# A graph layer on one core: TensorE takes over more of the gather, with 10 sets of nodes instead of 7 and index rows that come from DRAM

## The chip, the cores and the metric

The kernel runs on one core of a Trainium2 chip. The metric is the device time of one launch in microseconds (us); before the change it is 1440.02 us, the median of three runs (1439.52 to 1440.55).

The engines that matter: PE (TensorE, matrix products into PSUM), DVE (VectorE), ACT (ScalarE), POOL (GpSimd, which here issues indirect DMAs) and SP (SyncE, which issues ordinary DMAs). Each works through its own queue in order, and waits for the others by semaphores.

## What is computed

A layer of a graph network with 6250 nodes of 64 features and 206250 edges that are sorted by the node they lead to (`dst`):

```python
h = jnp.maximum(_layernorm(x, axis=-1), 0.0)
msg = jax.nn.relu(h[src] + edge_attr)
agg = jax.ops.segment_sum(msg, dst, num_segments=6250)
h = h + agg
h = jax.nn.relu(h @ W1 + b1)
out = x + h @ W2 + b2
```

The costly parts are `h[src]`, which picks 206250 rows of 256 bytes in no order, and the sum over the edges of each node.

## The kernel before

**Groups.** The edges are cut into 201 groups of 1024 (`NG`, `GE`) and a tail. A group is 128 partitions by 8 columns (`G`), so one column is 128 edges. The loop at L553 runs over the groups; two groups, an even and an odd one, are a pair `k`. The instructions stand in the order in which the code writes them; only semaphores let one engine run ahead of another.

**Two ways to gather.** For most columns POOL issues one indirect DMA each (`gather`, L156), which brings 128 rows of `h_rows` from DRAM into `xg`. In the pairs 2 to 99 (`K0`, `K1`) some columns are left to TensorE: 3 of 8 in even groups, 2 of 8 in odd ones (`EVEN`, `ODD`), `T = 5` per pair, 640 edges. This way goes in stages, a pair or two ahead of use:

- Once, at the start (`ranks`, L231): the source nodes of these edges are split into 7 parts (`SB`) of 7 blocks of 128 nodes, and each edge gets a place among the edges of its pair that have the same part. `hp` holds the node features in SBUF, as three bf16 pieces that add up to f32, 192 columns.
- `hold` (L377, DVE): a one-hot matrix from edge to place. `source` (L387, PE; L389, ACT): products with it give, for each place and part, the source node as a 16-bit number, with the places down the partitions.
- `spread` (L395, PE): transposes that turn a column of such numbers into a row that stands in every partition, in PSUM. It is done for the sources (7) and for the places of the edges, `spot` (5).
- `find` (L403, DVE): 7 comparisons of 128x896 that make the one-hot matrices `found`, from node to place. `back` (L410, DVE): 7 comparisons of 128x640 that make `backs`, from place to edge.
- `slots_of` (L417, PE; L421, ACT): 49 products of `found` with `hp`, added up per part, put the picked rows at their places, `picked`. `pick` (L439, PE): 7 products per column of `backs` with `picked` bring them to the edges, in PSUM beside a copy of the edge attributes (`room`, L430, ACT).

**Messages and sums.** `take` (L481, ACT) copies the attributes of a group to PSUM (`full`); `messages` adds the gathered rows (L489, DVE), folds the three pieces and the attributes of the picked columns into it (L491, DVE), and ACT applies the relu (L494). `one_hot` (L465, DVE) compares each edge's node, counted from the first of its group, with 64 numbers (`W`), and `window_sum` (L503, PE) adds the messages of a group into a window of 64 nodes. `sum_into_z` (L460, DVE) adds the window to `z`, two groups later (`LAG`). Whenever 512 nodes of `z` are done (`blocks_behind`), the two layers follow (L511, L524) and the result is stored (L534).

**Queues and buffers.** `load` issues the attributes on SP (L147) and the gathers on POOL for the next group. `ea` and `xg` have 10 buffers (`LOOK`), so POOL's queue can be up to ten groups ahead of the messages. Of the eight PSUM banks `rows` has one, `pick` two, `turned` two, and `wslots`, `full` and `agg` one each.

## Time and profile before

| | |
|---|---|
| profiled execution, whole run | 1440.22 us |
| its span, first to last instruction | 1438.5 us |
| mean granted TensorE clock | 0.958 |
| gathers (L156), us on POOL | 1036.8 from `h_rows`, 41.2 from `x` |
| `slots_of` (L417), us on PE | 487.7 for 4802 products |
| `pick` (L439), us on PE | 326.2 for 3430 products |
| `window_sum` (L503), us on PE | 234.8 for 3224 |
| `find` (L403), us on DVE | 414.1 for 686 comparisons, 675 ns each |
| `back` (L410), us on DVE | 322.6 for 686, 542 ns each |
| `hold` (L377) and `one_hot` (L465), us on DVE | 79.4 and 136.9 |
| mean traffic of the DMA engines | 71 GB/s |

The times of an engine's groups can be added up against the span; consecutive instructions overlap a little, so the mean duration times the count is more than the busy time. A line of the order of time gives the start in us from the span's start, the duration in us, the engine, the line of the kernel, the operation, the tiles written and read, how many were merged, and in brackets the idle time before it and what ended that. In the list of waits stand the waiting engine and line, the one waited for, the total in us, the number of times and the longest.

### The profile page before, as it was taken

The page shows a single profiled execution, that of the slowest core. Times are in us where ns is not written, and L with a number is a line of the kernel's source. Part 1 is how long each engine was busy: PE and PEld are TensorE (multiplying, and loading weights), DVE is VectorE, ACT ScalarE, POOL GpSimd, SP SyncE. Part 2 cuts the span into 40 slices and gives each one's busy share as a digit, 9 for nine tenths or more (in the row PEclk, how much of TensorE's full clock was granted, in tenths as well). Part 3 has the DMA queues.
Part 4 walks back from the last instruction along what each step waited for, and adds up shares of the span by engine and source line. Part 5 has one row for each costly group of instructions (what it writes and reads, how often), then busy time and mean ns, then how long its engine had stood idle before and what let it go on. Part 6 is the DMA issues. An engine that isn't in the chain of part 4 may idle for free. (4 is left out here: it accounts for less than half of the span.)

```text
span 1438.5 us, 34730 instructions
## 1 busy us (share of the span) xinstructions
PE 1150.1 (80%) x13824; PEld 1015.8 (71%) x13824; DVE 1298.3 (90%) x2546; ACT 478.2 (33%) x1253; POOL 1079.6 (75%) x1131
## 2 busy tenths in 40 slices
PE   1448788888888888888889888888878888888774
PEld 0237677877777777777778777777767777777773
DVE  6889999999999999999999999998988998999972
ACT  2323233333333333333333333333333333333331
POOL 7877777777777777777777777777777777777774
PEclk9959899999999999999999999999999999999995
DMA  5332213214214214214214214214213213311411
GB/s 174 75 98 64 59 29 105 75 28 120 68 28 119 61 28 126 60 28 123 57 28 127 61 28 126 54 28 119 68 28 111 68 29 101 82 32 33 129 28 24
DMA packets 80069, 101.68 MB, mean 71 GB/s; under 512 B 29692, under 2 KB 35964, under 8 KB 79900
## 3 DMA queue, kind: packets, MB, share of 16 engines
q0 software_dynamic: 35904, 36.84, 13.3%
q1 hardware_dynamic: 42748, 60.85, 13.2%
q8 instruction: 110, 1.80, 0.5%
q10 hardware_dynamic: 1248, 1.70, 0.3%
q14 instruction: 59, 0.48, 0.1%
HBM read 96.10 MB, written 3.20 MB: 69 GB/s over the span
## 5 line engine op out<-in xcount | busy, mean ns | idle before, releaser
L156 POOL DMA_INDIRECT xg<-h_rows,src_sb x1090 | 1036.8, 951 | 332.2 <-issue 279.2
L417 PE MATMUL rows<-hp,found 128*128 128x192 bf16 x4802 | 487.7, 250 | 27.7 <-DVE found L403 27.6
L417 PEld LDWEIGHTS <-found 128*128 128x128 bf16 x4802 | 390.7, 99 | 61.8 <-DVE found L403 44.8
L403 DVE TENSOR_SCALAR found<-turned,ids 128x896 bf16<-128x896 int16 x686 | 414.1, 675 | 2.1 <-PE turned L395 2.1
L439 PE MATMUL pick<-picked,backs 128*128 128x192 bf16 x3430 | 326.2, 251 | 111.0 <-ACT pick L430 110.3
L439 PEld LDWEIGHTS <-backs 128*128 128x128 bf16 x3430 | 296.8, 99 | 136.4 <-issue 124.2
L421 ACT CAST picked<-rows 128x384 bf16<-128x384 f32 (+1 forms) x392 | 170.8, 436 | 516.2 <-PE rows L417 513.0
L410 DVE TENSOR_SCALAR backs<-turned,ids 128x640 bf16<-128x640 int16 x686 | 322.6, 542 | 0.0
L503 PE MATMUL agg<-oh,msg 128*64 128x64 f32 x3224 | 234.8, 227 | 44.0 <-DVE z L460 43.5
L503 PEld LDWEIGHTS agg<-oh,msg 128*64 128x64 f32 x3224 | 206.7, 140 | 89.2 <-DVE z L460 57.9
L491 DVE TENSOR_REDUCE full<-pick 128x128 f32<-128x512 f32 (+1 forms) x294 | 179.6, 611 | 43.0 <-PE pick L439 4.8
L494 ACT ACTIVATE msg<-full 128x512 f32<-128x512 f32 x202 | 120.7, 598 | 198.9 <-DVE full L491 182.2
L489 DVE TENSOR_TENSOR full<-full,xg 128x320 f32<-128x320 f32 (+1 forms) x202 | 105.6, 523 | 56.0 <-DMA xg<-h_rows,src_sb 43.6
L465 DVE TENSOR_TENSOR oh<-slot,wslots 128x512 f32<-128x512 f32 x202 | 136.9, 678 | 0.0
L481 ACT COPY full<-ea 128x320 f32<-128x320 f32 (+1 forms) x202 | 92.7, 459 | 22.3 <-DMA ea<-in_edge_attr_dram 16.3
L377 DVE TENSOR_TENSOR holds<-place,wslots 128x640 bf16<-128x640 f32 x98 | 79.4, 811 | 0.0
L430 ACT COPY pick<-ea 128x128 f32<-128x128 f32 (+1 forms) x294 | 65.6, 244 | 0.0
L395 PE MATMUL turned<-ident_b,sources 128*128 128x128 bf16 x686 | 57.4, 227 | 6.5 <-ACT sources L389 5.2
L395 PEld LDWEIGHTS <-sources 128*128 128x128 bf16 x686 | 43.2, 101 | 18.8 <-ACT sources L389 5.5
L389 ACT CAST sources<-rows 128x7 int16<-128x7 f32 x98 | 16.4, 167 | 120.6 <-PE rows L387 113.3
L156 POOL DMA_INDIRECT xg<-in_x_dram,src_sb x32 | 41.2, 1287 | 11.0 <-issue 9.4
L395 PE MATMUL turned<-ident_b,spot 128*128 128x128 bf16 x490 | 45.0, 225 | 0.0
(99 smaller groups left out, 404.0 us busy)
## 6 DMA issues: line engine op xcount, KB each, us to landing
ea<-in_edge_attr_dram SPq DMA_DIRECT2D x201, 256.0 KB
xg<-h_rows,src_sb POOLq DMA_INDIRECT x1090
x_sb<-in_x_dram SPq DMA_DIRECT2D x4, 384.0 KB
h_rows<-ln_h SPq DMA_DIRECT2D x4, 384.0 KB
h_nodes<-h_rows SPq DMA_DIRECT2D x2, 768.0 KB
xb<-in_x_dram SPq DMA_DIRECT2D x12, 128.0 KB
out_dram<-o SPq DMA_DIRECT2D x12, 128.0 KB
dst_sb<-in_dst_main_dram ACTq DMA_DIRECT2D x1, 804.0 KB
```

Source lines behind the costliest of these rows:

```text
L156: nc.gpsimd.indirect_dma_start(out=xg[:, j, :], out_offset=None, in_=rows[:, :], in_offset=bass.IndirectOffsetOnAxis(ap=idx[:, j:j + 1], a ...
L395: nc.tensor.transpose(row[:, i], col[:, i:i + 1].bitcast(BF16).to_broadcast([P, P]), ident_b)
L403: nc.vector.tensor_scalar(found[k][:, b], row, ids[:, b:b + 1], None, op0=ALU.is_equal)
L410: nc.vector.tensor_scalar(backs[k][:, m], row, ids[:, m:m + 1], None, op0=ALU.is_equal)
L417: nc.tensor.matmul(ps[:, i], found[k][:, b, m + i, :], hp[:, (m + i) * SB + b].rearrange("p t d -> p (t d)"), start=(b == 0), stop=(b == S ...
L421: nc.scalar.copy(picked[k][:, m:m + n], ps[:, :n])
L439: nc.tensor.matmul(pk[:, u, :3].rearrange("p t d -> p (t d)"), backs[k][:, m, t0 + i + u, :], picked[k][:, m], start=(m == 0), stop=(m == ...
L465: nc.vector.tensor_tensor(oh[:, :n], slot[:, cols_of(g)].unsqueeze(2).to_broadcast([P, n, W]), wslots[:, :W].unsqueeze(1).to_broadcast([P, ...
L489: nc.vector.tensor_tensor(full[:, :m], full[:, :m], xg[:, :m], ALU.add)
L491: nc.vector.tensor_reduce(full[:, m + i:m + i + c], pk[:, :c].rearrange("p j t d -> p j d t"), AX.X, ALU.add)
L494: nc.scalar.activation(msg[:, :n], full[:, :n], AF.Relu)
L503: nc.tensor.matmul(pa, msg[:, j, :], oh[:, j, :], start=(j == 0), stop=(j == n - 1))
```

## The change

TensorE gets 4 columns of even groups and 2 of odd ones; POOL keeps 4 and 6. The nodes are split into 10 parts of 625, each 5 blocks of 125. The rows that are compared are no longer made by transposes into PSUM: the places (`spot`) of all pairs are turned once at the start and stored in DRAM, and the sources of a pair are computed with the places along the row, stored in DRAM, and read back into every partition, 16 bits each. `find` becomes 5 comparisons of 125x1280, `back` 10 of 128x768, `slots_of` 50 products, `pick` 10 per column. A small `mask` per pair (two operations on DVE) takes the place of the arrays `part_n` and `part_b`. The banks of `turned` go to `rows` (2) and `pick` (3). The window has 48 nodes, `slot` is 16-bit, the window starts are read 16 at a time. Loads enter six groups ahead (`AHEAD`), with nine buffers. In the loop the comparisons stand ahead of the messages.

The diff, cut to its core:

```diff
-W = 64
+W = 48
-LOOK = 10
+LOOK = 9
+AHEAD = 6
-SB = 7
-KB = SB * SB
-PART = SB * P
-EVEN, ODD = 3, 2
+SB, BB, BN = 10, 5, 125
+KB = SB * BB
+PART = BB * BN
+EVEN, ODD = 4, 2
-RV = 8
+RV = 16
...
     def ranks(pool):
...
-        for m in range(SB):
-            nc.vector.tensor_tensor(part_n[:, m], mine[:, m], src_f, ALU.mult)
-            nc.vector.tensor_tensor(part_b[:, m], mine[:, m], block, ALU.mult)
...
+        for c in range(0, KS * T, P):
+            n = min(P, KS * T - c)
+            turned = psum.tile([P, P], BF16, name="rows", bufs=2)
+            nc.tensor.transpose(turned[:n], spot[:, c:c + n].bitcast(BF16), ident_b)
+            sp = pool.tile([P, P], BF16, name="sp", bufs=2)
+            nc.scalar.copy(sp[:n], turned[:n])
+            nc.sync.dma_start(out=spot_rows[c:c + n, :], in_=sp[:n])
...
-    slot = const.tile([P, C + CT], F32, name="slot")
+    slot = const.tile([P, C + CT], I16, name="slot")
...
+    def mask(k):
+
+        at = hot.tile([P, T, SB], BF16, name="at", bufs=1)
+        nc.vector.tensor_tensor(at, part[:, k - K0].unsqueeze(2).to_broadcast([P, T, SB]),
+                                of_part.unsqueeze(1).to_broadcast([P, T, SB]), ALU.is_equal)
+        mk = hot.tile([P, T, 2, SB], BF16, name="mask")
+        nc.vector.tensor_tensor(mk, at.unsqueeze(2).to_broadcast([P, T, 2, SB]),
+                                node[:, k - K0].unsqueeze(3).to_broadcast([P, T, 2, SB]), ALU.mult)
+        masks[k] = mk
+
     def source(k):
 
-        oh = holds.pop(k)
-        ps = psum.tile([P, SB], F32, name="rows", bufs=1)
+        oh, mk = holds.pop(k), masks.pop(k)
+        ps = psum.tile([SB, P], F32, name="rows", bufs=2)
         for t in range(T):
-            for i, a in enumerate((part_n, part_b)):
-                nc.tensor.matmul(ps, oh[:, t, :], a[:, :, k - K0, t], start=(t + i == 0), stop=(t == T - 1 and i == 1))
-        sources[k] = hot.tile([P, SB], I16, name="sources")
-        nc.scalar.copy(sources[k], ps)
-
-    def spread(k, col, n):
-
-        row = psum.tile([P, SB, P], BF16, name="turned", bufs=2)
-        for i in range(n):
-            nc.tensor.transpose(row[:, i], col[:, i:i + 1].bitcast(BF16).to_broadcast([P, P]), ident_b)
-        return row
+            for i in range(2):
+                nc.tensor.matmul(ps, mk[:, t, i, :], oh[:, t, :], start=(t + i == 0), stop=(t == T - 1 and i == 1))
+        col = hot.tile([SB, P], I16, name="source")
+        nc.scalar.copy(col, ps)
+        line = dram.tile([SB, P], I16, name="source_row", bufs=3)
+        nc.sync.dma_start(out=line, in_=col)
+        sources[k] = hot.tile([P, SB * P], I16, name="sources")
+        nc.sync.dma_start(out=sources[k], in_=line.rearrange("(o m) s -> o (m s)", o=1).to_broadcast([P, SB * P]))
+
+    def spot(k):
+
+        spots[k] = hot.tile([P, T * P], BF16, name="spots")
+        nc.sync.dma_start(out=spots[k], in_=spot_rows[(k - K0) * T:(k - K0 + 1) * T, :]
+                          .rearrange("(o t) s -> o (t s)", o=1).to_broadcast([P, T * P]))
 
     def find(k):
 
-        row = spreads.pop((k, "source")).bitcast(I16)
-        found[k] = hot.tile([P, SB, SB, P], BF16, name="found")
-        for b in range(SB):
-            nc.vector.tensor_scalar(found[k][:, b], row, ids[:, b:b + 1], None, op0=ALU.is_equal)
+        row = sources.pop(k)
+        found[k] = hot.tile([P, BB, SB, P], BF16, name="found")
+        for b in range(BB):
+            nc.vector.tensor_scalar(found[k][:BN, b].rearrange("p m s -> p (m s)"), row[:BN], ids[:BN, b:b + 1], None,
+                                    op0=ALU.is_equal)
 
     def back(k):
 
-        row = spreads.pop((k, "spot"))[:, :T].bitcast(I16)
+        row = spots.pop(k).bitcast(I16)
         backs[k] = hot.tile([P, SB, T, P], BF16, name="backs")
         for m in range(SB):
-            nc.vector.tensor_scalar(backs[k][:, m], row, ids[:, m:m + 1], None, op0=ALU.is_equal)
+            nc.vector.tensor_scalar(backs[k][:, m].rearrange("p t s -> p (t s)"), row, ids[:, m:m + 1], None,
+                                    op0=ALU.is_equal)
...
+    for g in range(AHEAD):
+        enter(g)
     take(0)
+    for k in (K0, K0 + 1):
+        spot(k)
     hold(K0)
+    mask(K0)
     for g in range(NG + 1):
         k, even = g // 2, g % 2 == 0
+        now = is_set(k + 1)
+        enter(g + AHEAD)
         if g >= LAG:
             sum_into_z(g - LAG)
             blocks_behind(g - LAG)
+        if even:
+            if now:
+                slots_of(k + 1, 0, 2)
+                slots_out(k + 1, 0, 2)
+                back(k + 1)
+            if is_set(k + 2):
+                source(k + 2)
+            if is_set(k + 3):
+                spot(k + 3)
+        else:
+            if now:
+                slots_of(k + 1, 6, 2)
+                slots_out(k + 1, 6, 2)
+                slots_of(k + 1, 8, 2)
+                slots_out(k + 1, 8, 2)
+            if is_set(k + 2):
+                find(k + 2)
+            if is_set(k + 3):
+                hold(k + 3)
         if g < NG:
             room(g + 1)
         if g >= 1:
             window_sum(g - 1)
+        if now and even:
+            for m in (2, 4):
+                slots_of(k + 1, m, 2)
+                slots_out(k + 1, m, 2)
+        messages(g)
+        take(g + 1)
         if g < NG and is_set((g + 1) // 2):
             pick(g + 1)
+        if even and is_set(k + 3):
+            mask(k + 3)
         one_hot(g)
```

`slots_out` is the copy by ACT that stood at the end of `slots_of`. The lines that this order replaces are left out of the diff: before, `messages` and `take` stood ahead of `room` and `window_sum`, and `source`, `back`, `find` and `hold` after `pick`.

## The prediction

> **What bounds the kernel now.** I read the page's busy line first, then the groups by line and shape, then POOL's waits, then the order of time at the start, in the middle and at the end.
>
> ```profile
> PE 1150.1 (80%) x13824; PEld 1015.8 (71%) x13824; DVE 1298.3 (90%) x2546; ACT 478.2 (33%) x1253; POOL 1079.6 (75%) x1131
> L156 POOL DMA_INDIRECT xg<-h_rows,src_sb x1090 | 1036.8, 951 | 332.2 <-issue 279.2 <-DMA xg<-h_rows,src_sb 33.2 <-DVE found L403 11.0
> POOL xg L156 <- issue: 288.6, 947, 0.3
> ...
> 1420.68 0.94 POOL L156 DMA_INDIRECT xg<-h_rows,src_sb  x1 [0.30 <-issue]
> 1421.06 0.70 DVE L489 TENSOR_TENSOR full<-full,xg 128x512 f32<-128x512 f32 x1 [8.27 <-DMA xg<-h_rows,src_sb]
> ...
> 1423.18 0.94 POOL L156 DMA_INDIRECT xg<-h_rows,src_sb  x1 [0.30 <-issue]
> ```
>
> DVE has the largest share, yet POOL is the bound. A gather lies on POOL for 0.94 us and the next begins 0.30 us after it: a spacing of 1.249 us. No wait of POOL's own is longer than 0.3 us ("issue"), apart from one of 1.5 us at the start. The first gather starts at 4.50 us, the last ends at 1424.12. 1122 gathers (1090 + 32) at 1.249 make 1401.4 us; the stretch is 1419.6. So POOL is never free: 18.2 us of longer gathers are all that is left. DVE waits 8.27 us for gathered rows near the end. After the last gather come 14.4 us of tail (1438.5 - 1424.1), and the run of the profile took 1.7 us more than its span (1440.22 against 1438.5; the median of the runs, 1440.02, is the same within 0.02%).
>
> In quiet stretches DVE and PE turn a pair of groups in 12.61 us (`found` begins at 710.60 and 723.21), where POOL needs 11 gathers, 13.74 us. They work off the lead that POOL has at the start, and then wait.
>
> **Fewer gathers.** A pair goes from 11 gathers to 10; 98 pairs save 98 x 1.249 = 122.4 us on the engine that sets the end. 1024 gathers make 1279.0 us.
>
> **What DVE's new comparisons do to POOL.** This decides. `found` and `backs` read PSUM today, and the gathers beside them take 0.94 us. Afterwards they read 16-bit rows in SBUF and write SBUF. The loop of before has no such row, but its first 55 us do:
>
> ```profile
> 42.10 2.42 DVE L251 TENSOR_SCALAR mine<-part 128x490 bf16<-128x490 f32 x7
> 42.24 1.07 POOL L156 DMA_INDIRECT xg<-in_x_dram,src_sb  x1 [0.30 <-issue]
> 43.61 1.06 POOL L156 DMA_INDIRECT xg<-in_x_dram,src_sb  x1 [0.30 <-issue]
> ...
> 46.12 0.66 DVE L254 TENSOR_TENSOR part_n<-mine,src_f 128x490 bf16<-128x490 bf16 x1
> 46.24 8.90 POOL L156 DMA_INDIRECT xg<-in_x_dram,src_sb  x1 [0.31 <-issue]
> ...
> 53.65 0.67 DVE L255 TENSOR_TENSOR part_b<-mine,block 128x490 bf16<-128x490 bf16 x1
> ```
>
> Two kinds of streak, both SBUF to SBUF. Under seven tensor-scalars back to back (2.42 us) two gathers lose 0.12 us each: each is held to the end of the operation that was running and slips in before the next. Under fourteen tensor-tensors with two SBUF inputs one gather is shut out until the whole streak is over: 8.90 us instead of 0.94. The new comparisons are tensor-scalars, like L251; L254 is the other bound.
>
> Their length first. From 490 to 1612 f32 elements a tensor-scalar within SBUF goes from 0.413 us (L251) to 0.995 (L339): 0.52 ns an element and 0.16 us fixed. Out of PSUM, 16-bit elements run at 0.52 ns (L410 to L403: 542 to 675 ns for 256 more) where f32 runs at 1.05 (L465: 410 to 679 ns for 256 more). Halving the element halves its time there, so I take 0.26 ns for 16 bits in SBUF: 0.49 us for 1280 elements, 0.36 us for 768. Consecutive ones start some 0.07 us closer than they last (L403: 4.23 us for seven of 0.675), so `found` is 5 x 0.42 = 2.1 us (before 4.23) and `backs` 10 x 0.29 = 2.9 us (3.29). If nothing halves, they are 3.8 and 4.9 us.
>
> Now the loss of POOL per pair. By L251's share (0.244 of 2.42 us, 10%), 5.0 us of comparisons and 0.5 us of `mask` (two tensor-tensors with two SBUF inputs) cost 0.56 us. By half an operation for each gather that lands there (2.1/1.25 x 0.21 + 2.9/1.25 x 0.145 + 0.05) it is 0.74. I take 0.65, or 64 us in 98 pairs: both events of L251 met the operation at the same point, so neither figure is better. The ends: 0, and the L254 kind. There a gather meets a streak after 0.62 us on average and waits for the rest: (2.1 - 0.62) + (2.9 - 0.62) + 0.05 = 3.8 us per pair.
>
> The Trainium skill speaks against the change here ("SBUF — State Buffer", "Who interferes with whom"): a Vector operation in a two-port mode and a GpSimd operation shut each other out for the whole instruction, and tensor-scalars within SBUF can take that mode. Read so, all 5.0 us of comparisons would be lost to POOL in each pair and the sum below would come to about 1321 + 98 x 5.0 = 1811 us. The L251 rows contradict this reading: three more operations of the streak ran over the rest of the first gather, and it lost only 0.12 us.
>
> **DVE and PE, beside POOL.** DVE per pair after: `found` 2.1, `backs` 2.9, `holds` 0.95 (0.81 at 640 elements, 128 more at 1.05 ns), one-hot 2 x 0.54 (384 elements), window adds 0.38, `full` 0.43 + 0.55, three reductions of 0.70, `mask` about 0.47 (nearest row: L465 at 256 elements, 0.41): 11.0 us, counted as before's 13.0 (which turned in 12.61). PE: a stream of 128x192 matmuls advances by 0.082 us (21 in 1.89 us with 0.25 us for the last). 50 + 60 of them instead of 49 + 35 are 9.1 us, two window sums at most 2.3 (1.15 each today), twelve source matmuls of 128 columns 0.65 (transposes: seven in 0.55 us); 12 transposes leave. Sum 12.05, before 10.7. ACT has two more copies, 5.4 of 13 us. All lie below the 12.49 us that ten gathers take, so they are hidden while POOL is the bound; without this cover each 0.1 us on PE would cost 10 us. The same cover hides what is only moved: `backs` and `found` ahead of the messages (ACT's relu comes 2 to 3 us later in its step, and the window sum that reads it one step later), the second bank of rows, the third of picks, the 16-bit slots, the window starts read 16 at a time.
>
> PE and DVE also wait for each other, and a new path runs through DRAM: source matmuls, ACT's cast, a write, and behind it on SP's queue a read that spreads the row, then `found`. Landing events give 1.7 us for a store (out_dram at 767.60) and 2.9 for a 256 KB load. From the one-hot of an even group to the `found` that depends on it: 0.9 + 3.3 + 0.8 + 0.7 on PE (window sum, 40 picks, 10 slots, sources), 0.5 for the cast and what ACT does before it (an estimate), 4.7 for both transfers: 10.9 us, and one pair's period must be as long. That fits too. Behind a `found` that waits stand `holds`, the messages and the one-hot of its group on DVE, and for these ACT and PE's next window sum. Behind SP's waits stand the loads of edge attributes, which now enter six groups early; their late arrival today (ACT waits 16.3 us for them in total) goes, worth nothing while POOL sets the end.
>
> **The start.** The 7.95 us that L254 and L255 held a gather go with them; the other 10.3 us of long gathers I keep. New: nine buffers instead of ten, so POOL may be only 56 gathers ahead, done at about 4.5 + 70 + 5 = 80 us. Then it needs group 0's messages, which end at 87 today. The rank work gets about 5 us shorter on DVE, but the five stores of spot rows now stand in front of the two loads of `h_nodes` on SP's queue; these take 5.4 and 8.8 us to land, start some 11 us later than now, and DVE reaches group 0 some 4 us later. POOL waits from 80 to about 90, and a little again behind groups 2 and 3: 11 us (bounds 0 and 25).
>
> **Sum.** 4.5 + 1279.0 + 10.3 + 11 + 64 + 14.4 = 1383.2 us of span, and 1.7 outside: **1385 us**, 3.8% below the median before.
>
> **Rivals.**
> 1. *The streaks shut POOL out as L254 did* (slower). 3.8 us per pair instead of 0.65: 1385 + 309 = 1694 us. The break-even is (1440 - 1321)/98 = 1.2 us per pair. For it: the 8.90 us. Against it: L251 is of the right kind of instruction. 0.13.
> 2. *POOL isn't held at all*: 1385 - 64 = 1321; PE at 12.05 us per pair from the 119 us at which group 4 is reached, plus 25, comes to 1325. For it: after the first 160 us hardly any gather is long today. Against: L251. 0.16.
> 3. *Sixteen bits don't halve the time* (slower): DVE needs 11.0 + 1.7 + 2.0 = 14.7 us per pair, 119 + 98 x 14.7 + 25 = 1585. Against: L403's rate. 0.06.
> 4. *The path through DRAM becomes the bound*: if write and read take 7.4 us instead of 4.7 (the `h_nodes` load alone took 5.4 to 8.8), the period is 13.6 and the time 119 + 98 x 13.6 + 25 = 1477; it takes over above (1385 - 144)/98 = 12.7 us per pair. For it: it is in series with PE. 0.13, a fifth of it still below 1440.
>
> **How the numbers follow.** The forecast has 0.52; its own range is 1350 to 1425 (loss 0.3 to 0.95 us per pair, stall 0 to 25). With rival 2 and most of rival 4 the range is 1318 to 1480; rivals 1 and 3 (0.19) are left out. Faster by over 0.2%, which is about what a measurement of this kernel can tell: 0.52 + 0.16 + 0.02, or 0.70; slower 0.28, between them 0.02.
>
> **What would show it.** Right: 1024 gathers with POOL's waits at 0.3 us from about 120 us on; mean of a gather between 0.98 and 1.04 us; `found` near 0.49 and `backs` near 0.36 us each; POOL waiting once for about 10 us near 80 us; DVE waiting for xg. Wrong: gathers of 2 us and more under `found` and `backs` (rival 1), `found` near 0.82 us (3), DVE idle before `found` until a DMA (4), PE without gaps (2).

## The result, and the profile after it

The changed kernel takes 1623.53 us, the median of four runs (1617.59 to 1643.88), the kernel before 1439.77 us: a ratio of 1.126, with a 95% interval from 1.121 to 1.131. It is slower by 184 us, where 1385 us and a gain were forecast.

The profiled execution took 1643.88 us, its span is 1642.2. It is the slowest of the four, so the terms read from it below add up to 20 us more than the median. From its page, the busy line, the first lines of the chain, and the groups that answer to those shown of before (busy us and mean ns of one; then the engine's idle time before it and what ended most of it):

```profile
PE 1349.7 (82%) x15482; PEld 1255.1 (76%) x15482; DVE 1185.5 (72%) x2846; ACT 542.8 (33%) x1356; POOL 1271.6 (77%) x1034
...
POOL 39%; DMA 21%; issue 19%; DVE 12%; PE 7%; ACT 1%; DVEq 0%; POOLq 0%; SPq 0%; ACTq 0%
...
L158 POOL DMA_INDIRECT xg<-h_rows,src_sb x992 | 1236.2, 1246 | 344.0 <-issue 268.8
...
L435 DVE TENSOR_SCALAR backs<-spots,ids 128x768 bf16<-128x768 int16 x980 | 331.8, 407 | 0.0
...
L427 DVE TENSOR_SCALAR found<-sources,ids 125x1280 bf16<-125x1280 int16 x490 | 241.4, 554 | 64.6 <-DMA sources<-source_row 64.3
L519 DVE TENSOR_TENSOR full<-full,xg 128x256 f32<-128x256 f32 (+1 forms) x202 | 100.3, 496 | 254.8 <-DMA xg<-h_rows,src_sb 241.1
```

POOL is still the bound: it leads the chain, from 142 us on the next gather begins 0.32 us after the last at most, and DVE's largest wait is for gathered rows (241 us at L519). But a gather from `h_rows` takes 1246 ns on the mean instead of 951, although its median is 0.945 (before 0.944). 98 fewer of them are outweighed by longer ones. Of the 303 us by which all gathers together exceed 0.944 us each, 295 lie in the 410 gathers that overlap `found` or `backs`. Before the change 744 gathers overlapped these comparisons, which then read PSUM, and lost 1 us in all.

The loss isn't spread evenly. 113 gathers are longer than 1.5 us (from 115 us on), and these alone lose 277 us, 2.45 us each. Two stretches of the order of time show both kinds:

```profile
725.01 0.55 DVE L495 TENSOR_TENSOR oh<-slot,wslots 128x384 f32<-128x384 int16 x1
725.08 0.94 POOL L158 DMA_INDIRECT xg<-h_rows,src_sb  x1 [0.30 <-issue]
725.47 0.19 DVE L490 TENSOR_TENSOR z<-z,agg 64x48 f32 x1
...
728.82 1.01 POOL L158 DMA_INDIRECT xg<-h_rows,src_sb  x1 [0.30 <-issue]
729.15 2.42 DVE L427 TENSOR_SCALAR found<-sources,ids 125x1280 bf16<-125x1280 int16 x5 [3.50 <-DMA sources<-source_row]
730.13 1.10 POOL L158 DMA_INDIRECT xg<-h_rows,src_sb  x1 [0.30 <-issue]
...
804.34 3.93 POOL L158 DMA_INDIRECT xg<-h_rows,src_sb  x1 [0.30 <-DVE full L521]
804.66 0.19 DVE L490 TENSOR_TENSOR z<-z,agg 64x48 f32 x1
804.77 3.37 DVE L435 TENSOR_SCALAR backs<-spots,ids 128x768 bf16<-128x768 int16 x10
...
808.57 0.94 POOL L158 DMA_INDIRECT xg<-h_rows,src_sb  x1 [0.30 <-issue]
```

A run of comparisons on DVE without idle time between them is called a streak here. At 804.34 a gather is under way when `backs` begins, and ends 0.13 us after the last of the ten comparisons: it was held for the whole streak. At 728.82 a gather also meets the start of a streak and takes 1.01 us; the one that starts inside the streak takes 1.10. What differs stands on DVE ahead of the streak. At 804.77 the first comparison begins 0.11 us after the add into `z` (`sum_into_z`, L490), while that add still runs; at 729.15 DVE had been idle for 3.50 us.

This holds for the whole execution. I took every gather that began between 0.56 us before a streak's start and 0.30 us after it:

| streak | what stands before it on DVE | such gathers | held (over 1.3 us) |
|---|---|---|---|
| `backs`, 10 | the add into `z`, no idle time | 50 | 44 |
| `found`, 5 | the add into `z`, no idle time | 37 | 36 |
| `found`, 5 | the add into `z`, then idle time | 27 | 0 |

Seven more met a streak behind the last add of a block's output (L563), three of them without idle time; none was held.

The second loss is at the start. POOL has used its nine buffers at 81 us and waits 28 us for DVE:

```profile
66.15 4.23 SPq L287 DMA_DIRECT2D spot_rows<-sp  x5
70.56 18.48 SPq L312 DMA_DIRECT2D h_nodes<-h_rows  x3
81.96 1.52 ACT L315 CAST hp<-h_nodes 125x1600 bf16<-125x1600 f32 x1 [11.87 <-DMA h_nodes<-h_rows]
83.52 1.82 DVE L316 TENSOR_TENSOR h_nodes<-h_nodes,hp 125x1600 f32<-125x1600 f32 x1 [17.93 <-ACT hp L315]
...
109.29 0.99 POOL L158 DMA_INDIRECT xg<-h_rows,src_sb  x1 [28.02 <-DVE at L395]
```

The `h_nodes` loads are issued behind the five stores of `spot_rows`, and the first takes 11.4 us from its issue to ACT's first use of it (70.56 to 81.96). With smaller gaps until 140 us, POOL waits 41.6 us in all.

One thing is needed to read the times below: the experiments ran on five other chips than the two kernels above, in six series (e to j, by the first letter of a run). There the kernel before took 2012 to 2153 us, PE pauses beside POOL's gathers (last section), and POOL waits for the others (532 us in i4), so it isn't the bound there. What carries over is how long gathers and other operations take. The total times don't: those of the kernel before scatter by 3 to 7% within a series, and kernels that ran in two of them change sides. e2 and f2 are the same kernel on the same chip: 2114.6 us against 2019.9 for the kernel before in one series, 2000.8 against 2139.8 in the other.

### The profile page after: what moved, and what is told of

The parts are those of the page before. It is cut to its first block, busy times and chain, and to the rows that moved or that the text cites. A ratio compares the mean times of both kernels' runs of the same rounds, so it can differ in the third digit from the quotient of the medians.

```text
span 1642.2 us, 38789 instructions
## 1 busy us (share of the span) xinstructions
PE 1349.7 (82%) x15482; PEld 1255.1 (76%) x15482; DVE 1185.5 (72%) x2846; ACT 542.8 (33%) x1356; POOL 1271.6 (77%) x1034
## 4 chain that ended last, share of the span: by engine, by line
POOL 39%; DMA 21%; issue 19%; DVE 12%; PE 7%; ACT 1%; DVEq 0%; POOLq 0%; SPq 0%; ACTq 0%
POOL xg L158 39%; DMA xg<-h_rows,src_sb 16%; DVE found L427 2%; PE pick L469 2%; PE rows L443 2%; DVE backs L435 2%; DMA sources<-source_row 1%; DVE full L521 1%; DMA h_nodes<-h_rows 1%; PE agg L533 1%; DVE holds L388 1%; DVE full L519 1%; DMA source_row<-source 1%; PE rows L408 1%; DMA ea<-in_edge_attr_dram 0%
## 5 line engine op out<-in xcount | busy, mean ns | idle before, releaser
L158 POOL DMA_INDIRECT xg<-h_rows,src_sb x992 | 1236.2, 1246 | 344.0 <-issue 268.8
L469 PE MATMUL pick<-picked,backs 128*128 128x192 bf16 x5880 | 552.7, 255 | 0.1
L469 PEld LDWEIGHTS <-backs 128*128 128x128 bf16 x5880 | 512.6, 102 | 10.2
L443 PE MATMUL rows<-hp,found 125*128 125x192 bf16 x4900 | 481.4, 255 | 0.7 <-DVE found L427 0.3
L443 PEld LDWEIGHTS <-found 125*128 125x128 bf16 x4900 | 422.5, 101 | 22.7 <-issue 11.3
L533 PE MATMUL agg<-oh,msg 128*64 128x48 f32 x3224 | 247.6, 235 | 163.8 <-ACT full L511 76.5
L435 DVE TENSOR_SCALAR backs<-spots,ids 128x768 bf16<-128x768 int16 x980 | 331.8, 407 | 0.0
L451 ACT CAST picked<-rows 128x384 bf16<-128x384 f32 x490 | 229.5, 478 | 297.4 <-PE rows L443 294.3
L427 DVE TENSOR_SCALAR found<-sources,ids 125x1280 bf16<-125x1280 int16 x490 | 241.4, 554 | 64.6 <-DMA sources<-source_row 64.3
L519 DVE TENSOR_TENSOR full<-full,xg 128x256 f32<-128x256 f32 (+1 forms) x202 | 100.3, 496 | 254.8 <-DMA xg<-h_rows,src_sb 241.1
L521 DVE TENSOR_REDUCE full<-pick 128x128 f32<-128x512 f32 x294 | 205.7, 700 | 30.9 <-DVE full L521 0.9
L460 ACT COPY pick<-ea 128x128 f32<-128x128 f32 x294 | 71.5, 270 | 0.0
L490 DVE TENSOR_TENSOR z<-z,agg 64x48 f32 x202 | 38.4, 190 | 40.9 <-issue 21.9
L541 PE MATMUL rows<-z,w_sb 64*64 64x512 f32 (+1 forms) x26 | 16.9, 737 | 36.6 <-ACT full L511 19.5
```

The costliest lines, as they stand in the source:

```text
L158: nc.gpsimd.indirect_dma_start(out=xg[:, j, :], out_offset=None, in_=rows[:, :], in_offset=bass.IndirectOffsetOnAxis(ap=idx[:, j:j + 1], a ...
L427: nc.vector.tensor_scalar(found[k][:BN, b].rearrange("p m s -> p (m s)"), row[:BN], ids[:BN, b:b + 1], None, op0=ALU.is_equal)
L435: nc.vector.tensor_scalar(backs[k][:, m].rearrange("p t s -> p (t s)"), row, ids[:, m:m + 1], None, op0=ALU.is_equal)
L443: nc.tensor.matmul(ps[:, i], found[k][:BN, b, m + i, :], hp[:BN, (m + i) * BB + b].rearrange("p t d -> p (t d)"), start=(b == 0), stop=(b ...
L451: nc.scalar.copy(picked[k][:, m:m + n], halves.pop((k, m)))
L469: nc.tensor.matmul(pk[:, u, :3].rearrange("p t d -> p (t d)"), backs[k][:, m, t0 + i + u, :], picked[k][:, m], start=(m == 0), stop=(m == ...
```

## The experiments

The runs of the layer together. "Held" counts gathers over 1.5 us after 115 us, "lost" what these exceed 0.944 us by, "all" what all gathers after 115 us exceed it by; "before" is the kernel before in the same series. Times are medians of all executions.

| run | held | lost, us | all, us | median, us | before, us |
|---|---|---|---|---|---|
| changed kernel, first chip | 113 | 277 | 299 | 1623.5 | 1439.8 |
| i4_changed_again | 62 | 175 | 193 | 2078.7 | 2152.9 |
| e4_start, f3_start (one kernel) | 60, 67 | 170, 186 | 187, 204 | 2124.4, 2067.0 | 2019.9, 2139.8 |
| e1_break, f1_break (one kernel) | 17, 19 | 33, 37 | 57, 61 | 2154.7, 2107.1 | 2019.9, 2139.8 |
| e2_woven, f2_woven (one kernel) | 23, 38 | 21, 31 | 84, 101 | 2114.6, 2000.8 | 2019.9, 2139.8 |
| f4_woven_start | 37 | 29 | 98 | 1989.1 | 2139.8 |
| h2_own_wait, h3_own_wait_start | 63, 64 | 178, 179 | 192, 193 | 2089.0, 2062.7 | 2139.2 |
| i2_one_gap, i3_one_gap_start | 46, 45 | 125, 126 | 142, 144 | 2085.0, 2076.0 | 2152.9 |
| j1_swap, j2_swap_start | 61, 59 | 174, 173 | 192, 189 | 2068.8, 2080.5 | 2125.1 |
| e3_no_gather | - | - | - | 1421.9 | 2019.9 |

The changed kernel holds fewer gathers there than on the first chip (62), because `found` mostly waits for its `sources` first: in i4 85 of the 92 that follow the add into `z` begin after idle time, and none of the 46 gathers that meet those is held, while 53 of 53 are held at `backs` directly behind the add. The totals that were expected of e1 to j2 presumed a chip on which the kernel before takes 1440 us, or said so where they didn't; they can't be judged here, except that of e3.

### What PE, DVE, ACT and the path through DRAM take without gathers

```diff
-        gather(xg, src_sb[:, cols_of(g)], pool_cols(g), x if g < RAW else h_rows)
+        if not is_set(g // 2):
+            gather(xg, src_sb[:, cols_of(g)], pool_cols(g), x if g < RAW else h_rows)
...
-        nc.vector.tensor_tensor(full[:, :m], full[:, :m], xg[:, :m], ALU.add)
+        rows_g = none if is_set(g // 2) else xg
+        nc.vector.tensor_tensor(full[:, :m], full[:, :m], rows_g[:, :m], ALU.add)
```

> The changed kernel without any gather by POOL in the pairs 2 to 99: messages of these groups add a constant tile instead of the gathered rows; everything else stays. It shows what PE, DVE, ACT and the path through DRAM take by themselves. Theory A (POOL is the bound of the changed kernel): far faster, 119 + 16 (later start) + 98 x 12.2 + 25 = 1355 us (1320 to 1400). Rival D (PE with 12.05 us per pair, or the path through DRAM, has become the bound): about 1600 us.

Measured: 1421.94 us, 0.711 of the kernel before in that series (0.701 to 0.721), above the 1320 to 1400 of theory A and far below rival D's 1600. From its page:

```profile
PE 1278.0 (90%) x15482; PEld 1194.8 (84%) x15482; DVE 1171.9 (82%) x2846; ACT 555.1 (39%) x1356; POOL 47.0 (3%) x54
...
L432 DVE TENSOR_SCALAR found<-sources,ids 125x1280 bf16<-125x1280 int16 x490 | 235.2, 546 | 96.3 <-DMA sources<-source_row 96.0
```

From the first `found` (127.5 us) to the last (1385.7) a pair takes 12.97 us on the mean. By the starts of the `source` products 65 of the 97 periods are 12.2 us, and the chain of 700 to 727 us, two of these, is PE's products one behind the other. The others are longer, up to 27 us, mostly near the layers of a block, and in one of them, from 243 us on, the chain runs through `sources` and DVE. PE is busy for 98% of the time from 200 to 1380 us. So the changed kernel's other half has little room left even with gathers that cost nothing. On the first chip, where the first `found` is at 111.2, the same arithmetic gives 111.2 + 97 x 12.97 + 35 = 1404 us (an estimate; 35 us is what e3 takes after its last `found`). POOL alone, without the held gathers, would be at 1642.2 - 295 = 1347.

### Breaking the streaks

A memset of 128x1 after each comparison (e1, f1), or the comparisons spread between DVE's other work (e2, f2):

```diff
+            nc.vector.memset(gap[:, m:m + 1], 0.0)
```

> The changed kernel with one tiny memset (128x1, SBUF) after every comparison of found and backs. Theory A (a gather that asks while SBUF-to-SBUF comparisons run back to back is shut out until the whole streak ends, because DVE hands over from one to the next without letting go): the 113 gathers of over 1.5 us, 277 us in the profile of the changed kernel, disappear; a gather under the comparisons loses at most one operation (0.46 us), some 60 us in all: 1400 us (1370 to 1440). Rival B (each such comparison shuts POOL out for its own length, whatever stands between): POOL loses as much as before or more, 1600 us or over. Rival C (the longer gathers come from the extra row traffic, 150 MB against 102): no change, 1620 us.

> The changed kernel with a write of 128x1 f32 by DVE (a memset) after each of the fifteen comparisons of a pair, and nothing else; the same as e1_break, once more, to have it where the kernel before takes about 1440 us. Theory A (a gather that has to touch a port in the middle of a streak of comparisons without a gap is shut out until the streak ends; the small operation, which doesn't take that port, lets it in): the 113 long gathers (over 1.5 us) fall below 40, the time lost by gathers under the streaks falls from 295 us to 60-120, and the time from 1624 to 1420-1490 us. Theory B (each comparison shuts POOL out, streak or not): long gathers stay about 110 and the time at 1600-1650. Theory D (the path of PE and DVE, 1422 us without gathers in e3_no_gather, takes over): not below 1420.

```diff
-                back(k + 1)
+                turn[0] = back(k + 1)
+                some(3)
...
-            if is_set(k + 2):
-                find(k + 2)
...
+            if is_set(k + 2):
+                turn[0] = find(k + 2)
+                some(1)
```

Here `find` and `back` yield after each comparison, and `some(n)` lets the next n go ahead: three after the add into `z`, two after the add into `full`, two after each reduction.

> The changed kernel with the comparisons spread between the other DVE operations of the same group, so that no streak is longer than three (two masks apart); no instruction added or removed. Theory A: gathers are held 1.0 us at most, on average much less; 1400 us (1370 to 1450). Rivals B and C: 1620 us as before, since the same comparisons and the same traffic remain.

> The changed kernel with the comparisons spread between DVE's other work in streaks of at most three, instead of five and ten; nothing is added. Theory A: a gather waits at most for the rest of three comparisons (1.0 us for backs, 1.4 for found) and most for none, long gathers below 30, 60-100 us lost instead of 295, 1420-1480 us. Theory B: the loss goes by the number of comparisons, not by their grouping: 1600-1650 us. Theory D: not below 1420 us; and as found is ready later in its step, PE may wait for it, which would hold it at up to 1500 with gathers that are short.

Both cut what gathers over 1.5 us lose to a fifth or less (from 170-186 us to 33-37 and 21-31). But the woven streaks of two and three hold a gather for less than that, so all gathers together still lose 84 and 101 us there, half of the 187 and 204 of e4 and f3, and 57 and 61 with the memsets; f2's 38 long ones are more than the 30 expected at most. The same comparisons and the same row traffic remain in e2, so rivals B and C of e1 fall. The totals don't tell what that is worth: e1 is at 1.070 of before (1.043 to 1.098) and e2 at 1.058 (1.027 to 1.089), e4 below at 1.060 (1.036 to 1.084). e2 and f2 also show who holds: of the gathers that meet the three comparisons behind the add into `z` 75 of 84 are held in f2, of those behind the add into `full` 49 of 51, of those behind a reduction out of PSUM 0 of 69. In this order the add into `full` follows the add into `z` and its three comparisons without a pause of DVE, so what it does by itself can't be read here.

### The start

```diff
-            nc.sync.dma_start(out=spot_rows[c:c + n, :], in_=sp[:n])
+            nc.scalar.dma_start(out=spot_rows[c:c + n, :], in_=sp[:n])
...
+                for a, b in ((0, 112), (112, BN)):
+                    nc.sync.dma_start(out=h[a:b, :n], in_=rows_k[a:b])
```

> The changed kernel with the start alone altered: the five stores of spot rows on ACT's queue instead of ahead of the h_nodes loads on SP's, and each h_nodes load cut into 112 and 13 partitions. In the changed kernel POOL waits 28 us at 81 us for group 0 and 41.6 us in five gaps. If these gaps lie on the path that sets the end: 25 us less, 1598 us (1590 to 1610). If POOL's lead makes them free: 1620 us.

> The changed kernel with a shorter start: the five stores of spot_rows are issued by ACT instead of standing before the h_nodes loads on SP's queue, and each h_nodes load is cut into 112 and 13 partitions. If POOL's wait of 28 us at 81 us comes from those stores and the slow loads, and POOL sets the end: that gap falls to 10-18 us and the time to 1605-1615 us. If the streaks are all that counts and the gap is refilled elsewhere: 1620-1625 us.

> Both edits of f2_woven and f3_start. If POOL is still the bound when the long gathers are gone, they add up: f2_woven less what f3_start gains, 1400-1465 us. If the path of PE and DVE is the bound then (theory D), the earlier start of group 0 is gained all the same, since that path begins there: 1395-1460. If f2_woven is held by neither (found late on DVE), no difference to f2_woven beyond 20 us.

POOL's longest wait near the start is shorter with these edits in every series:

| series | with the edits | without |
|---|---|---|
| e | 35.9 us (e4) | 47.7 (e1), 51.4 (e2) |
| f | 33.2 (f3), 31.3 (f4) | 36.5 (f1), 49.8 (f2) |
| h | 25.6 (h3) | 40.8 (h2) |
| i | 25.1 (i3) | 37.2 (i2), 37.8 (i4) |
| j | 35.7 (j2) | 36.6 (j1) |

The gain is from 1 to 19 us, and two edits stand together in it. ACT, which now issued the stores, waited 4.82 us in f3 for one of them before it could begin with `h_nodes`. The loads themselves became faster: from the issue of the first large one to the last packet of the second it is 16.8 us in i4 (93.3 to 110.1) and, cut into 112 and 13 partitions, 9.7 in e4 (90.4 to 100.1). The traces also show the 4-byte packets with which a load ends: 5 for each in the changed kernel, 29 for its two parts in e4, and 16 for each in the kernel before. f4 has the lowest median of the runs with gathers on those chips, 1989.06 us (1972.81 to 1999.70) beside 2139.75 (2086.32 to 2169.76) for the kernel before in its series; f2 and f3 are below that too, but, as said, the same kernels were above it in the other. Where the kernel before takes 1440 us none of them was run.

### Streaks alone

None of the layer: 60 gathers per stage, and 16 streaks of one kind on DVE, each followed by four reductions out of PSUM. The 60 gathers are over after 75 to 82 us if none is held, so only the first streaks of a stage have gathers beside them.

```python
for i in range(16):
    run()
    for r in range(4):
        reduce()
```

> A measurement by itself: none of the layer is computed (the output is x), POOL issues 60 gathers of 128 rows of x per stage without a wait, and beside them DVE runs, 16 times per stage, a streak of one kind of operation and then four reductions out of PSUM of about 0.7 us. Ten stages, named by the tile that the gathers write: xa no streak; xb five comparisons of 125x1280 within SBUF, 16 bit (found); xc ten of 128x768 (backs); xd the same ten with a 128x1 memset after each; xe three of them; xf one; xg twenty; xh seven of 128x896 out of PSUM (found before); xi eight of 128x490 from f32 in SBUF to bf16 (like L251 of before); xj seven tensor-tensors of 128x490 bf16 with two SBUF inputs (like L254 of before). Theory A (a gather that has to touch a port inside a streak without a gap is shut out until the streak ends): gathers near 0.95 us in xa and xh; time lost per streak about 1.0-1.4 us in xb, 1.5-2 in xc, 3-5 in xg (the longest gather about 7 us, the length of the streak), 0.1-0.5 in xd and xe, below 0.1 in xf; xj the worst for its length. xi like xc for its length if all tensor-scalars within SBUF act alike, or 0.1-0.3 us per streak if f32 operands leave room, as the two gathers of L251 had it. Theory B (each comparison shuts POOL out by itself, streaks or not): xd loses what xc does, xe three tenths of it, xf a tenth (0.15-0.2 us per comparison).

> As g1_streaks (none of the layer is computed), but each comparison of a streak has an output of its own. In g1_streaks the outputs took turns in two buffers, so that from the third on each comparison waited on a semaphore for the one two before it; no comparison of the changed kernel does that, and no gather of g1_streaks was shut out. Stages: xa ten of 128x768 without such a wait; xb ten with it, as before; xc five of 125x1280; xd ten with a memset of 128x1 after each; xe three; xf twenty; xg seven out of PSUM; xh eight of 128x490 from f32; xi seven tensor-tensors; xj five of 128x768; all but xb without a wait. Theory A2 (a streak shuts a gather out only where no comparison in it waits on a semaphore): gathers over 1.5 us in 8 to 14 of the 16 streaks of xa, each until the streak ends; 1.5-2 us lost per streak in xa, 1-1.4 in xc, 3-5 in xf with gathers of up to 7 us, 0.5 in xj, 0.1-0.3 in xb, xd and xe, 0 in xg. Theory E (what shuts gathers out in the layer isn't in DVE's stream alone, but needs PE's and ACT's traffic or the gathered rows' place in DRAM): xa like xb, no gather over 1.5 us in either.

No streak within SBUF held a gather to its end, not even the one of twenty: of all 144 gathers of g1 and h1 that began between 0.56 us before a streak and 0.30 us into it none took over 1.3 us. The time lost beside 9 streaks of ten was 2.6 us in g1 and 1.7 in h1 (with and without waits between the comparisons), beside 3 and 6 of twenty 4.7 and 2.7, beside 14 and 15 of five `found` 5.3 and 5.5, beside 14 of eight from f32 7.7 (longest gather 1.6 us), beside 9 out of PSUM 0.1 and 0.0. So theory A fell as I had put it, and A2 with it. The tensor-tensors of L254's kind held none either (longest gathers 1.09 and 1.18 us). h2 had the layer's comparisons wait for each other, and says the same:

```diff
-        for m in range(SB):
+        for m in (0, 5, 1, 6, 2, 7, 3, 8, 4, 9):
+            n = T * P + (EX if m not in (4, 9) else 0)
```

> The changed kernel with comparisons that wait for each other: their order is 0, 3, 1, 4, 2 and 0, 5, 1, 6, 2, 7, 3, 8, 4, 9, and all but the last of each run write 4 elements into the block of the one two later, which writes them anew and so waits for it; sources and spots stand in two fixed buffers each, 4 elements longer. No work is added. Theory A2: gathers over 1.5 us after 115 us fall from 113 (60 to 67 where the kernel before takes 2000 us and more) to below 15, as in g1_streaks, and the time from 1624 to 1400-1450 us, bounded from below by the 1422 us of e3_no_gather's chain with its late start. Theory E: long gathers as before, no gain.

> h2_own_wait with the shorter start of f3_start. Theory A2: 10-25 us less than h2_own_wait, 1385-1440 us; theory E: 10-25 us less than the changed kernel.

63 and 64 held: no change. Something in the layer was missing in the stages, and sorting the changed kernel's gathers by what precedes a streak gave the table in the section on the result.

### What stands before the streak

The same stages, with one more operation directly ahead of each streak, such as `z_add` of 64x48:

```python
nc.vector.tensor_tensor(zs[:D, :48], zs[:D, :48], bank[:D, :48], ALU.add)
streak(10)
```

> As h1_streaks_free (none of the layer is computed), but each streak is preceded by one more operation of DVE that runs into it without idle time: xa a 64x48 f32 add of SBUF and PSUM into SBUF (like sum_into_z), then ten comparisons of 128x768; xb the same with a 128x1 memset between; xc that add before seven comparisons of 128x896 out of PSUM (as before the change); xd a 128x256 add of PSUM and SBUF into PSUM (like the add into full); xe a 128x384 comparison of SBUF and PSUM (like one_hot); xf a 64x48 add within SBUF; xg the add of xa, then a reduction, then ten; xh a 64x48 copy out of PSUM; xi the add before three; xj the add before twenty. Theory F (the trace of the changed kernel: of 87 gathers that met a streak directly behind the add into z 80 were held until its end, of 27 that met one after idle time none; woven: 49 of 51 behind the add into full, none of 69 behind a reduction): a gather is held if its access falls into the first comparison after an add of SBUF and PSUM that ran into it without a gap, and then until the streak's end. So long gathers in xa, xd, xi (1.5 us at most) and xj (up to 7.5 us), about 5 to 10 of 16 streaks each; none in xb, xc, xg; xe, xf and xh open: xe like xd if it is the kind of operands. Theory E (PE's and ACT's traffic is needed): no gather over 1.5 us anywhere.

| stage | ahead of the streak | streak | streaks beside gathers | gathers that met the start | of these over 1.3 us | longest gather | lost |
|---|---|---|---|---|---|---|---|
| xa | add 64x48, SBUF and PSUM | 10 | 16 | 15 | 15 | 4.10 us | 48.7 us |
| xf | add 64x48 within SBUF | 10 | 16 | 16 | 16 | 4.10 | 49.2 |
| xh | copy 64x48 out of PSUM | 10 | 16 | 16 | 16 | 4.11 | 49.2 |
| xi | add of xa | 3 | 16 | 16 | 16 | 1.79 | 12.2 |
| xj | add of xa | 20 | 16 | 16 | 16 | 7.39 | 101.8 |
| xb | add of xa, memset | 10 | 14 | 10 | 3 | 3.70 | 11.4 |
| xg | add of xa, reduction | 10 | 8 | 6 | 1 | 3.86 | 4.6 |
| xc | add of xa | 7 out of PSUM | 8 | 6 | 0 | 0.95 | 0.1 |
| xd | add 128x256 into PSUM | 10 | 8 | 7 | 0 | 1.14 | 2.0 |
| xe | comparison 128x384 (`one_hot`) | 10 | 8 | 4 | 0 | 1.12 | 2.0 |

The last reduction of the four stands ahead of the operation in the second column. Gathers that met the start are those that began between 0.56 us before it and 0.30 us into the streak, as in the section on the result. xa, xi and xj held gathers as theory F had it, though in 15 or 16 streaks instead of 5 to 10; xd, which it expected like xa, did not, and xb and xg have four held gathers where it expected none.

The order of time in the stages xa, xg and xj:

```profile
17.70 0.18 DVE L131 TENSOR_TENSOR zs<-zs,bank 64x48 f32<-64x48 f32 x1
17.81 3.37 DVE L124 TENSOR_SCALAR big<-half,ids 128x768 bf16<-128x768 int16 x10
17.91 4.10 POOL L186 DMA_INDIRECT xa<-in_x_dram,src_sb  x1 [0.30 <-issue]
...
765.28 0.70 DVE L177 TENSOR_REDUCE some<-full 128x128 f32<-128x512 f32 x1
765.37 0.95 POOL L186 DMA_INDIRECT xg<-in_x_dram,src_sb  x1 [0.30 <-issue]
765.89 3.58 DVE L124 TENSOR_SCALAR big<-half,ids 128x768 bf16<-128x768 int16 x10
766.62 1.02 POOL L186 DMA_INDIRECT xg<-in_x_dram,src_sb  x1 [0.31 <-issue]
...
1120.06 7.24 POOL L186 DMA_INDIRECT xj<-in_x_dram,src_sb  x1 [0.30 <-issue]
1120.40 0.18 DVE L131 TENSOR_TENSOR zs<-zs,bank 64x48 f32<-64x48 f32 x1
1120.51 6.66 DVE L124 TENSOR_SCALAR big<-half,ids 128x768 bf16<-128x768 int16 x20
```

This is the layer's behaviour without the layer, and it excludes theory E. One short operation on 64x48 elements, at the end of which the first comparison starts, and a gather that meets the start is held to the streak's end: 0.76 us lost per streak of 3, 3.05 of 10, 6.36 of 20. With a reduction between, the gathers at 765.37 and 766.62 pass the same streak in 0.95 and 1.02 us. The 64x48 operation reads PSUM or SBUF and may be a copy: that makes no difference. And the same add ahead of comparisons out of PSUM (xc) costs nothing; in the kernel before nearly all streaks moreover stood behind a reduction.

A gather and a streak keep step in these stages, so the sixteen cases are repeats of few: in xa seven gathers began 0.46 us before the streak, seven 0.10 us into it, one 0.32 us before it. The position isn't what decides: in xb six gathers at the first two of these positions passed in 0.99 to 1.14 us behind the memset, and in stage xa of h1 four that began 0.33 to 0.37 us before the streak passed in 0.94 behind a reduction. For xd and xe the positions are fewer and others, so their zeros say less.

### Taking the contact away in the layer

One memset per streak (i2, i3), with the changed kernel beside it (i4); then the add into `z` ahead of `one_hot`, so that `one_hot` stands before the streak (j1, j2):

```diff
         backs[k] = hot.tile([P, SB, T, P], BF16, name="backs")
+        nc.vector.memset(gap[:, 1:2], 0.0)
```

```diff
-            sum_into_z(g - LAG)
...
+        if g >= 1:
+            sum_into_z(g - 1)
         one_hot(g)
```

> The changed kernel with one memset of 128x1 per streak, between the add into z and the first comparison: 196 operations of 60 ns, nothing else. Theory F: gathers over 1.5 us after 115 us fall from 113 (67 in f3_start on a chip where the kernel before takes over 2000 us) to below 8, the time lost under the streaks to 30-60 us, and the time from 1624 to 1400-1450 us, no faster than the 1422 us of e3_no_gather by more than 20. Theory A (each streak without a gap shuts out; then only a gap after each comparison helps, as in f1_break): long gathers fall by a fifth at most, as the streaks stay nine and four comparisons long.

> i2_one_gap with the shorter start of f3_start. Theory F: 10-25 us less than i2_one_gap, 1385-1430 us, below the kernel before; with theory A 1600 or more.

> The changed kernel itself, as the measure for i2 and i3 on the same chip: 1624 us and 113 long gathers, or, where the kernel before takes 2000-2140 us, 2060-2130 us and 60-70 long gathers.

> The changed kernel with two operations of DVE exchanged: the add into z stands ahead of one_hot of the same step instead of behind it, so that the comparisons follow one_hot (0.54 us) and not the add (0.19 us). Nothing is added or left out. Theory F, as i1_what_before sharpened it (held to the streak's end is what meets a streak that follows a short operation on SBUF, not one behind one_hot): gathers over 1.5 us after 115 us fall from 113 (60 to 67 where the kernel before takes 2000-2150 us) to below 10, all the time lost by gathers to 25-50 us; 1400-1450 us where the kernel before takes 1440, 2040-2085 where it takes 2150, since there the gathers aren't what sets the end. Theory A: no change in the long gathers.

> j1_swap with the shorter start of f3_start, the version that should beat both kernels: with theory F 1385-1430 us where the kernel before takes 1440, 10-25 us less than j1_swap elsewhere. If holding one_hot behind the add (which waits for PE) costs more than the exchange gains, it shows here as long waits of DVE before the add into z and no gain over the changed kernel.

The memset took away a quarter (62 to 46; theory F had said below 8), less than in xb; the exchange nothing (61; below 10 had been expected). In j1, in order of time:

```profile
1017.70 0.20 DVE L490 TENSOR_TENSOR z<-z,agg 64x48 f32 x1 [1.53 <-PE agg L533]
1017.82 0.54 DVE L495 TENSOR_TENSOR oh<-slot,wslots 128x384 f32<-128x384 int16 x1
1018.14 3.64 POOL L158 DMA_INDIRECT xg<-h_rows,src_sb  x1 [0.30 <-issue]
1018.29 3.37 DVE L435 TENSOR_SCALAR backs<-spots,ids 128x768 bf16<-128x768 int16 x10
```

The gather starts 0.3 us into `one_hot` and is held all the same. In j1 and j2 that befell 102 of the 119 gathers that met `backs` directly behind `one_hot` (49 of 58, 53 of 61). The add stands one operation further back, and DVE doesn't pause in between. Either the add's effect lasts through `one_hot`, or `one_hot` has it too. Stage xe speaks for the first: there `one_hot` stood behind a reduction, and the three gathers that began 0.11 to 0.21 us before the streak passed in 0.95 to 0.97 us, while in j1 and j2 all 19 that began 0.08 to 0.26 us before it were held. Three cases don't settle it. The totals are those of the kernel before: 0.9996 of it (0.982 to 1.018) and 1.009 (0.997 to 1.021). What these versions would take where the kernel before takes 1440 us wasn't measured. Nor did a run put the whole streaks behind a reduction, where f2's streaks of two and three held none of 69 gathers.

## Why the prediction was wrong

By its own terms, in us of the profiled span:

| term | forecast | measured |
|---|---|---|
| start to first gather, 1024 gathers at 1.249 | 4.5 + 1279.0 | 4.8 + 1279 |
| other long gathers | 10.3 | 8 |
| POOL held by comparisons | 64 | 295 |
| POOL waiting at the start | 11 | 41 |
| tail | 14.4 | 14.0 |
| sum | 1383.2 | 1642.2 |

**The step that failed is "What DVE's new comparisons do to POOL".** It had both rows: two gathers under L251 that lost 0.12 us each, and one under L254 that lost 7.95. It put the difference down to the kind of instruction and took L251's share, because the new comparisons are tensor-scalars like it. i1 shows that the same tensor-scalar streak does either, by what DVE did just before: 1.0 us gathers behind a reduction, the full streak behind a short operation; and in the changed kernel none of 27 was held behind idle time. The measured loss is 3.0 us per pair (295/98), nearer to the upper bound of 3.8 than to the 0.65 taken, and the mechanism is that of rival 1 with a condition that I had not seen. Nor is it the kind of instruction: seven tensor-tensors like L254 behind reductions held no gather (longest 1.18 us). The lines named there as its refutation came: gathers of 2 us and more under `found` and `backs`. What could have warned: a bound from two rows of opposite behaviour, one of them seen once and the other twice, was decided on one attribute of them; nothing was asked about their neighbours on DVE, though the order of the loop was in the diff (the comparisons were put directly behind `sum_into_z`). In the trace of before the two rows have different neighbours, and L254's is a short operation that ran until the streak began:

```profile
41.73 0.44 DVE L248 TENSOR_SCALAR block<-block 128x490 f32<-128x490 f32 x1
42.10 2.42 DVE L251 TENSOR_SCALAR mine<-part 128x490 bf16<-128x490 f32 x7
...
45.98 0.23 DVE L196 SCALAR_TENSOR_TENSOR ln_h<-ln_xc,ln_v 106x64 f32<-106x64 f32 x1 [0.51 <-DVE ln_v L194]
46.12 0.66 DVE L254 TENSOR_TENSOR part_n<-mine,src_f 128x490 bf16<-128x490 bf16 x1
```

The Trainium skill ("SBUF — State Buffer", "Who interferes with whom") says that the first to issue gets the shared ports for the whole instruction, and that a tensor-reduce never contends. The second agrees with the 0.95 us at 765.37. The first is too harsh for the streaks of h1, in which several comparisons run during one gather of 1.02 us, and too mild for xj, where one gather waits through twenty instructions. The forecast rejected the rule on the first count and had no reason left to fear the second.

**The start was mis-sized**: 41 us for 11. The order of events was right (nine buffers used at 81 us, forecast 80; stores before loads), but the loads themselves were taken at their old 5.4 to 8.8 us, and the first took 11.4. They now have 125 partitions instead of 128, and from the issue of the first large one to the last packet of the second it is 19.6 us (70.6 to 90.2) where it was 8.6 (52.3 to 60.9). The Trainium skill ("DMA: Bandwidth & Descriptors", on why a DMA increments its semaphore by 16) says that a transfer uses as many engines as the largest number up to 16 that divides the slowest dimension on both its sides; by that section it would be 5 for 125, an estimate. The trace agrees: each of these loads ends with 5 packets of 4 bytes, where those of 128 partitions ended with 16.

**What held.** POOL remained the bound, the other engines' waits on it included; 98 gathers went; sixteen bits halve the time per element (0.26 ns between 768 and 1280 elements). `found` and `backs` take 540 and 405 ns at the median and follow each other by 463 and 329 (forecast 490, 360, 420 and 290): the fixed part was too small by some 40 to 50 ns, 0.6 us per pair of DVE's time, which its waits for gathered rows cover.

**The cover was thinner than forecast.** PE was to need 12.05 us per pair, below POOL's 12.49. e3 has 12.2 in two pairs of three, so this price was near, but 12.97 on the mean, with the longer pairs near the layers. So the forecast of 1385 would have been missed by some 20 us without any held gather, by the 1404 us estimated there. Rival 4's path through DRAM at 13.6 us per pair isn't the bound of e3: DVE waits 96 us for `sources` in all, while in most pairs PE sets the period.

## What to carry to other kernels

Where an engine can hold up the one that sets the end, price an operation together with what runs ahead of it without a pause: the same streak of ten sixteen-bit comparisons within SBUF cost POOL 0.2 us behind a reduction (1.7 us beside 9 streaks, h1) and 3.05 us behind a 64x48 add. When two rows of a trace disagree by a factor of 66 (7.95 and 0.12 us), the row is not yet understood, and a range that leaves out one of them has to say what excludes it. Taking an engine's operands from PSUM to SBUF can halve its own time and still lose, if it then meets another engine that before it never met.

## What the runs showed of the hardware that was not expected

A gather on POOL can be held by DVE over twenty instructions and take 7.39 us (stage xj), and whether it is depends on an operation of 0.18 us directly ahead of the first of them. It has to meet the start: of the 91 gathers of the changed kernel that began 0.5 us or more behind the start of `backs` none took over 1.1 us. In xa a held gather ends 0.12 us after the streak if it began before it (3.95 us from 0.46 us before), and 0.82 us after it if it began in it (4.10 us from 0.10 us in). Why a short operation ahead has this effect, and what in it counts, its length, its 64 partitions or its few elements, no run shows.

On the five later chips PE pauses beside gathers. In j1_swap 5880 products of `pick` have 226 us of gaps before them, of which 108 are waits for ACT's copy (`pick`, L460) and 117 have no cause that the profile shows ("issue"); in e3_no_gather, without gathers, they have none. The first line is from the page of j1, the second from that of e3:

```profile
L469 PE MATMUL pick<-picked,backs 128*128 128x192 bf16 x5880 | 630.1, 268 | 225.8 <-issue 116.9
```

```profile
L474 PE MATMUL pick<-picked,backs 128*128 128x192 bf16 x5880 | 521.5, 247 | 0.0
```

The granted clock is 0.835 in the one and 0.962 in the other. i4 is the kernel of the first chip, and shows the same within one run: from 200 us on, of successive products of `slots_of` and `pick` (pauses over 3 us left out) 5.6% start more than 0.3 us after the one before while a gather is on POOL, 8.0% in the 2.5 us behind one, and 1.5% later than that; on the first chip, where the clock was 0.910, it is 1.6% beside gathers. There the kernel with fewer gathers comes out faster in one series in spite of the held ones (lowest executions 2059.0 us for i4 against 2098.8 for the kernel before) and slower in another (2104.5 for e4 against 1987.4), and on the first chip it is the slower. Which of the two behaviours a chip shows can't be read from the kernel.
